# Attention layer: VectorE's checks reordered around the degrees, with four adj buffers; rank-decay layer: counts of two blocks made ahead of the layer norm

## The chip, the cores and the metric

The kernel runs on one core of a Trainium2 chip. The metric is the device time of one execution in microseconds (us), shown as the median of three runs. A separate, profiled execution gives the trace from which all durations below are read.

## The reference

Four graph layers run in a row over 3327 nodes with 64 features and one adjacency matrix `adj` of zeros and ones. Each layer takes `h = relu(layernorm(x))` and adds its result to `x`.

```python
# layers 0 and 3: hyperbolic attention
adj_att = sigmoid(left[:, None] + right[None, :] + b) * adj
support = einsum('ij,ijd->id', adj_att, logmap(x[:, None], x[None, :]))
x = x + proj(expmap(x, support))
# layer 1: rank decay. The last 100 neighbours of a row count, each further one half as much
rank = cumsum(adj != 0, axis=1); deg = rank[:, -1:]; k = minimum(deg, 100)
w = mask * where(rank - (deg - k) > 0, 0.5 ** (k - pos), 0)
x = x + w @ (h @ weight) + bias
# layer 2: signed attention between two GRU cells, without the diagonal of adj
node_support = concat((A > 0) @ h, (A < 0) @ h)
x = x + d_edge * gru(node_support, h) + d_node * gru(gat(h, A, A), h)
```

For an adjacency of zeros and ones the attention of layer 2 becomes a sum over neighbours, scaled by a function of the node's degree. The kernel computes that short form, and checks beside it, on VectorE, that the matrix holds nothing but zeros and ones: it counts the zeros of each quarter block (`zeros`, line 1247) and adds the ones that it counts anyway. If the total is wrong, a general form of all layers runs afterwards. It doesn't run on this input.

## The kernel before

The 3327 nodes are padded to 26 blocks of 128. The matrix comes in transposed, as `adjT`. The program goes through the four layers one after the other. Layers 0 and 3 are `hyperbolic_series` (line 322), layer 1 is `plain_decay` (1273), layer 2 is `plain_gat` (1431).

**Order of the work.** Most of the work stands in blocks with an order written out by hand (`tc.manual_schedule(engines=...)`): inside such a block the named engines carry out their instructions in program order. Between blocks a planner decides; an instruction that nothing holds back may be put ahead of an earlier block's. One example matters: `table_of(f)` (line 117) loads a table of ScalarE functions by a tiny activation into the tile `spare`. The one on line 404, the first ScalarE instruction of layer 3's block, stands in ScalarE's queue amid layer 2, directly behind the `table_of` of line 1506. DMAs are issued by SyncE (SP) in its own queue; the load of a tile waits there until the buffer is free.

**Rank-decay layer.** The matrix is read in 52 steps `(c, b)`, a half of the columns each and 26 blocks of rows from the last to the first. A step reads one tile of 128x1664 floats (832 KB, `load`, seven buffers). VectorE turns it into an fp8 mask (`make_mask`, line 1326) and counts its zeros (1329, by line 1248), except for the thirteen steps listed in `LATE` (line 1240), whose zeros are counted in the next layer. The masks stay on chip for layers 2 and 3. For each of the two halves `o` of a step, TensorE adds to the running counts (`counts(k, o, after)`, line 1333), ScalarE makes the weights `2^-count` (`weights`, 1339), and TensorE completes the count (`counts(k, o, rest)`). `sums` (1350) multiplies the weights with `h`. The order is: masks of steps 0 and 1; the layer norm (`norm_relu`, 123: VectorE with two Squares on ScalarE, line 135, and `split2`, line 181); then the loop over steps (1386). `late` splits the other half of `h`. GpSimd adds the bias (1415) from step 3 on.

**Attention layer.** The thirteen tiles of `LATE` are read again into three `adj` buffers (1451 to 1455). After the layer norm, TensorE runs through the 26 blocks `b` from 25 to 0, 16 matmuls each (1518), into four banks `acc`. Between the blocks stand, by the table `todo`: `turn` (transposes of `h` and copies on ScalarE, 1476), `degrees(k)` for the four parts k (two matmuls that sum the diagonal, and a VectorE subtraction from `deg`, 1495), and `inverse` (1497): VectorE clamps `deg`, ScalarE takes Relu, Ln and Exp of it, and two VectorE instructions (1507, 1508) make the attention's factor in `deg`. Behind each even block VectorE gets one check, a zero count of one `LATE` tile. Then the GRUs run in eight units `u` (two cells by four column parts): `take(k)` (two copies on ScalarE, 1538, and a multiplication on VectorE, 1539), `take2` (1544), `products` (TensorE, 1553 and 1558), `sigmoids` (ScalarE, 1565), `before_tanh` (VectorE, 1571 and 1572), `tanh` (1575) and `state` (VectorE, 1582 to 1586).

**End of layers 0 and 3** (line 689 on): some fifty VectorE instructions on 128x26 tiles. In layer 3 `th` holds a tanh, a table of Sqrt is loaded behind it by an activation that reads `th` (740), and line 742 multiplies `th` in place.

Of the kernel before, what the change touches and what calls it, by code (L numbers as in the profile page):

```python
# [9 lines left out]
F32 = mybir.dt.float32  # L10
BF = mybir.dt.bfloat16
# [8 lines left out]
P = 128  # L20
T = 26
# [25 lines left out]
def tile_gnn4(ctx: ExitStack, tc: tile.TileContext, x, adjT, att0, b0, w1, bias1, w_gat, a_gat,  # L47
# [274 lines left out]
    def hyperbolic_series(r, params, ok, masks=None, done=None):  # L322
# [18 lines left out]
        with ExitStack() as st:  # L341
# [347 lines left out]
            with tc.tile_pool(name="hse", bufs=1) as tp:  # L689
# [28 lines left out]
                if r is None:  # L718


                    f = MIN_NORM
                    by, g = new("by"), new("g")
                    V.tensor_scalar(by, v2, -f * f, 1.0, op0=OP.mult, op1=OP.add)
                    V.tensor_scalar(g, by, MIN_NORM, None, op0=OP.max)
                    V.reciprocal(g, g)
                    V.tensor_mul(t, root, g)
                    A.activation(th, t, AF.Tanh)
                    V.tensor_mul(th, th, rr)
                    V.tensor_mul(y2, th, th)
                    stt(vh, vh, 2.0 * f, th, op0=OP.mult, op1=OP.mult)  # L730
                    V.tensor_mul(y2, y2, x2)
                    stt(d, v2, f * f, y2, op0=OP.mult, op1=OP.mult)
                else:

                    V.tensor_scalar(t, v2, 1e-8, None, op0=OP.max)
                    ti = inverse_root(tp, t, "ti")
                    V.tensor_mul(t, t, ti)
                    V.tensor_scalar(t, t, um, None, op0=OP.max)
                    A.activation(th, t, AF.Tanh)
                    table_of(AF.Sqrt, th[:, :1])  # L740
                    V.reciprocal(ti, t)
                    V.tensor_mul(th, th, ti)
                    V.tensor_mul(y2, th, th)
                    stt(vh, vh, 2.0, th, op0=OP.mult, op1=OP.mult)
                    V.tensor_mul(y2, y2, v2)
                    V.tensor_mul(d, y2, x2)
# [526 lines left out]
    def plain_decay(masks, zo, deg, wt, bias, gru, ball_of_r):  # L1273
# [11 lines left out]
        with ExitStack() as st:  # L1285
# [24 lines left out]
            with tc.tile_pool(name="pdacc", bufs=1, space=PSUM) as pa, tc.manual_schedule(  # L1310
# [11 lines left out]
                def make_mask(k):  # L1322
                    c, b = steps[k]
                    adj = adjs.pop(k)
                    mask = masks[b // 2].rearrange("p q (o s i) -> p q o s i", o=2, s=2)[:, b % 2, :, c, :]
                    V.tensor_scalar(mask, adj, 1.0, None, op0=OP.is_equal, saturate=False)  # L1326
                    if k not in LATE:
                        same = wk.tile([P, 2, CW], BF, name="same", bufs=1)
                        zeros(same, adj, zo[:, k:k + 1])
# [33 lines left out]
                        A.activation(outP[:, c * CW + h * BK:c * CW + (h + 1) * BK], acc[h], AF.Copy, scale=1.0 / SH)  # L1363


                K_ = len(steps)
                make_mask(0)
                make_mask(1)
                H = pers.tile([P, T, D], F32, name="H")

                def late():
# [9 lines left out]

                with tc.tile_pool(name="pdp", bufs=1) as tp:
                    norm_relu(tp, H, order=(1, 0), then=after_norm)
                for o in range(2):
                    cnt[o] = pa.tile([P, 2, 512], F32, name=f"cnt{o}")
                for k in range(K_ + 2):
                    c, b = steps[min(max(k, 0), K_ - 1)]
                    if 0 <= k < K_:
                        counts(k, 0, after)
                        weights(k, 0)  # L1390
                    if 0 <= k - 1 < K_:
                        counts(k - 1, 1, rest)
                        if steps[k - 1][1] == 0:
                            degrees(steps[k - 1][0], 1)
                    if 0 <= k < K_:
                        counts(k, 1, after)
                        weights(k, 1)
                    if 0 <= k - 1 < K_:
                        sums(k - 1)
                        if steps[k - 1][1] == 0:  # L1400
                            out_of(steps[k - 1][0])
                    if 0 <= k < K_:
                        counts(k, 0, rest)
                        if b == 0:
                            degrees(c, 0)
                    if k + 2 < K_:
                        make_mask(k + 2)
                        if k + AHEAD < K_:
                            load(k + AHEAD)
                    if k == 1:  # L1410
                        late()
                    if 3 <= k < 3 + T // 2:

                        ts = slice(2 * (k - 3), 2 * (k - 2))
                        G.tensor_tensor(X[:, ts, :], X[:, ts, :], bias[:, None, :].to_broadcast([P, 2, D]), op=OP.add)
                    if k == 3:
                        for _, bt, brz in gru:
                            G.tensor_tensor(brz, bt[:, :3], bt[:, 3:], op=OP.add)
                        ball_of_r()
                    if k in (T + 3, T + 6):  # L1420
                        t0 = k - T - 3
                        pt = pa.tile([P, 3, 2, D], F32, name=f"acc{t0 // 3}", bufs=2)
                        from_pairs(None, outP, add, wt, range(t0, t0 + 3), pt)
                    if k - 2 >= T:
                        b = steps[k - 2][1]
                        drop_diagonal(masks[b // 2][:, b % 2, :], b, 0, NP)
# [4 lines left out]
    def plain_gat(masks, zo, deg, first, wg, gru):  # L1431
# [8 lines left out]
        with ExitStack() as st:  # L1440
# [7 lines left out]
            wgT = pers.tile([D, D], F32, name="wgT")  # L1448
            hundred = pers.tile([P, 1], F32, name="hundred")
            V.memset(hundred, -100.0)  # L1450
            wk = st.enter_context(tc.tile_pool(name="pgl", bufs=3))
            late = []
            for k in LATE:
                late.append(wk.tile([P, 2, CW], F32, name="adj"))
                nc.sync.dma_start(late[-1], quarters(k))
            with tc.tile_pool(name="pgp", bufs=1) as tp, tc.tile_pool(name="pgacc", bufs=1, space=PSUM) as pa, \
                    tc.manual_schedule(engines={mybir.EngineType.Activation, mybir.EngineType.DVE,
                                                mybir.EngineType.PE}):
                def bank(k):
                    return pa.tile([P, 512], F32, name=f"bank{k}")  # L1460

                hn = tp.tile([P, T, D], F32, name="hn")
                norm_relu(tp, hn, H.rearrange("p k o d -> p o k d"), order=(1, 0),
                          then=lambda o: split2(*[p[:, :, o, :] for p in parts], H[:, :, o, :]))
# [20 lines left out]
                        for o in range(2):  # L1485
                            A.activation(xh[g][o][D:, cs], pt[o * D:(o + 1) * D, :n * P], AF.Copy)

                def degrees(k):

                    cs = slice(k * BK, (k + 1) * BK)  # L1490
                    dg = bank(6 + k % 2)[:, :BK]
                    for o in range(2):
                        PE.matmul(dg[o * D:(o + 1) * D, :], ones_bf[:, :D],
                                  diag[:, o * HP + k * BK:o * HP + (k + 1) * BK], start=True, stop=True)
                    V.tensor_sub(deg[:, cs], deg[:, cs], dg)

                def inverse():

                    few = hn.rearrange("p t d -> p (t d)")
                    r0 = tp.tile([P, T, D], F32, name="ln_sq").rearrange("p t d -> p (t d)")  # L1500
                    V.tensor_scalar(zo[:, 2 * T:], zo[:, 2 * T:], first, None, op0=OP.mult)
                    V.tensor_scalar(deg, deg, 1.0, None, op0=OP.max)
                    A.activation(few, deg, AF.Relu, bias=hundred, accum_out=ok[:, 3:])
                    A.activation(r0, deg, AF.Ln)
                    A.activation(r0, r0, AF.Exp, scale=-1.0)
                    table_of(AF.Sigmoid, r0[:, :1])
                    V.scalar_tensor_tensor(deg, deg, -1.0, r0, op0=OP.mult, op1=OP.mult)
                    V.scalar_tensor_tensor(deg, deg, 2.0, r0, op0=OP.add, op1=OP.mult)

                todo = {T - 4: lambda: turn(0), T - 6: lambda: degrees(0), T - 8: lambda: turn(4),  # L1510
                        T - 9: lambda: degrees(1), T - 11: lambda: turn(8), T - 12: lambda: degrees(2),
                        T - 14: lambda: turn(12), T - 15: lambda: degrees(3), T - 17: inverse}
                for b in range(T - 1, -1, -1):
                    mask = masks[b // 2][:, b % 2, :]
                    for i, w in enumerate([p[:, b % C2, b // C2, :] for p in parts]):
                        for k in range(C):
                            for o in range(2):
                                PE.matmul(acc[k][o * D:(o + 1) * D, :], w,  # L1518
                                          mask[:, o * HP + k * BK:o * HP + (k + 1) * BK],
                                          start=b == T - 1 and i == 0, stop=b == 0 and i == 1)  # L1520
                    if b in todo:
                        todo[b]()
                    if b % 2 == 0:
                        same = wk.tile([P, 2, CW], BF, name="same", bufs=1)
                        k = LATE[(T - 1 - b) // 2]
                        zeros(same, late.pop(0), zo[:, k:k + 1])

# [171 lines left out]
```

## Time and profile before

| | |
|---|---|
| median of three runs | 819.15 us (817.87 to 821.02) |
| profiled execution | 818.34 us, its span 816.6 us |
| VectorE (DVE) busy | 709.1 us, 87% of the span |
| TensorE (PE) / ScalarE (ACT) / GpSimd (POOL) busy | 659.8 / 576.2 / 416.1 us |
| layer 0, rank-decay layer | to 283.8 us; 283.9 to 428 us |
| attention layer, layer 3 | 428 to 531 us; 531 to the end |

Times in the trace are counted from the start of the span. A line of the timeline gives start, duration, engine, source line, operation, tiles, count, and in brackets the idle time of the engine before it with what ended it. In the lists of waits the columns are: who waited, on whose instruction, total us, times, longest. "issue" is time in which an engine waited for nothing that the profile shows.

### The profile page before, as it was taken

The page shows a single profiled execution, that of the slowest core. Times are in us where ns is not written, and L with a number is a line of the kernel's source. Part 1 is how long each engine was busy: PE and PEld are TensorE (multiplying, and loading weights), DVE is VectorE, ACT ScalarE, POOL GpSimd, SP SyncE. Part 2 cuts the span into 40 slices and gives each one's busy share as a digit, 9 for nine tenths or more (in the row PEclk, how much of TensorE's full clock was granted, in tenths as well). Part 3 has the DMA queues.
Part 4 walks back from the last instruction along what each step waited for, and adds up shares of the span by engine and source line. Part 5 has one row for each costly group of instructions (what it writes and reads, how often), then busy time and mean ns, then how long its engine had stood idle before and what let it go on. Part 6 is the DMA issues. An engine that isn't in the chain of part 4 may idle for free. (4 is left out here: it accounts for less than half of the span.)

```text
span 816.6 us, 11802 instructions
## 1 busy us (share of the span) xinstructions
PE 659.8 (81%) x4215; PEld 252.1 (31%) x4215; DVE 709.1 (87%) x985; ACT 576.2 (71%) x729; POOL 416.1 (51%) x296
## 2 busy tenths in 40 slices
PE   0799999999999049989993995427999999999960
PEld 0522233333332024435441651214222333333320
DVE  6789999989998899998967567996899999999976
ACT  2678888878886367777782575255888888888862
POOL 2299988989987050003120000004687777787730
PEclk9989999999999569999996997757999999999995
DMA  3567676776664739998913541001001001000001
GB/s 75 164 203 219 205 212 184 205 213 196 196 189 120 292 131 327 372 379 298 367 36 132 187 151 50 1 4 45 1 1 34 1 1 36 1 1 2 1 2 46
DMA packets 57621, 107.84 MB, mean 132 GB/s; under 512 B 8752, under 2 KB 33488, under 8 KB 57552
## 3 DMA queue, kind: packets, MB, share of 16 engines
q1 hardware_dynamic: 53200, 106.97, 40.5%
q10 hardware_dynamic: 4352, 0.02, 0.3%
q8 instruction: 35, 0.57, 0.3%
q14 instruction: 34, 0.28, 0.1%
HBM read 103.72 MB, written 0.88 MB: 128 GB/s over the span
## 5 line engine op out<-in xcount | busy, mean ns | idle before, releaser
L595 ACT ACTIVATE y<-slot,shift_c 128x768 f32<-128x768 f32 (+1 forms) x208 | 197.4, 949 | 68.4 <-ACT sig L575 48.6
L601 DVE TENSOR_TENSOR sig<-slot,sig 128x768 f32<-128x768 f32 (+1 forms) x208 | 213.2, 1025 | 23.3 <-POOL sig L577 2.1
L600 DVE SCALAR_TENSOR_TENSOR slot<-y,slot 128x768 f32<-128x768 f32 (+1 forms) x208 | 212.1, 1020 | 9.1 <-ACT y L595 9.0
L577 POOL TENSOR_TENSOR sig<-adj,sig 128x768 f32<-128x768 f32 (+1 forms) x104 | 201.9, 1962 | 28.1 <-ACT sig L575 26.0
L575 ACT ACTIVATE sig<-leftB,right 128x768 f32<-128x768 f32 (+1 forms) x208 | 204.1, 981 | 3.5 <-DVE bh L544 3.5
L577 POOL TENSOR_TENSOR sig<-mask,sig 128x768 f32<-128x768 fp8e4 (+1 forms) x104 | 174.6, 1680 | 61.6 <-ACT sig L575 57.6
L610 PE MATMUL slot<-sig,Xr 128*64 128x384 f32 (+1 forms) x832 | 188.3, 541 | 16.8 <-DVE sig L601 16.8
L588 PE MATMUL slot<-XC,XT 128*128 128x384 f16 (+1 forms) x416 | 142.9, 344 | 5.2 <-DVE sig L601 3.5
L589 PE MATMUL slot<-XF,XE 73*128 73x384 f16 (+1 forms) x416 | 142.0, 341 | 0.0
L1339 ACT ACTIVATE w<-cnt,ebias 128x832 bf16<-128x832 f32 x104 | 93.7, 950 | 30.7 <-PE cnt L1333 30.7
L1248 DVE TENSOR_SCALAR_CACHE_REDUCE same<-adj 128x1664 bf16<-128x1664 f32 x52 | 97.5, 1876 | 3.6 <-DMA adj<-in 3.4
L618 PE MATMUL slot<-sig,X 128*32 128x384 f32 (+1 forms) x832 | 96.0, 533 | 0.0
L610 PEld LDWEIGHTS slot<-sig,Xr 128*64 128x64 f32 x832 | 43.1, 135 | 122.5 <-DVE sig L601 83.4
L1333 PE MATMUL cnt<-mask,after 128*128 128x416 fp8e4 x208 | 54.8, 347 | 22.7 <-DVE mask L1326 19.8
L588 PEld LDWEIGHTS <-XT 128*128 128x128 f16 x416 | 40.8, 98 | 96.1 <-issue 70.7
L191 POOL TENSOR_TENSOR mask<-mask,offdiag 128x128 fp8e4<-128x128 fp8e4 x26 | 15.0, 594 | 97.9 <-PE cnt L1333 97.9
L1333 PE MATMUL cnt<-mask,rest 128*128 128x416 fp8e4 x208 | 54.7, 345 | 10.2 <-ACT w L1339 10.2
L400 POOL MEMSET X<- 128x832 f32 x2 | 1.6, 794 | 115.0 <-PE pt L1234 115.0
L1326 DVE TENSOR_SCALAR mask<-adj 128x1664 fp8e4<-128x1664 f32 x52 | 52.9, 1035 | 0.0
L589 PEld LDWEIGHTS <-XE 73*128 73x128 f16 x416 | 40.9, 98 | 33.6 <-issue 9.9
L1350 PE MATMUL acc<-w,h 128*64 128x416 bf16 x416 | 46.6, 345 | 0.0
L1518 PE MATMUL bank<-mask,h 128*64 128x416 fp8e4 x416 | 39.7, 348 | 0.0
(299 smaller groups left out, 521.8 us busy)
## 6 DMA issues: line engine op xcount, KB each, us to landing
adj<-in SPq DMA_DIRECT2D x65, 832.0 KB, 6.6
adj<-in SPq DMA_DIRECT2D x78, 384.0 KB, 3.9
adj<-in SPq DMA_DIRECT2D x27, 512.0 KB, 4.4
leftB<-left SPq DMA_DIRECT2D x6, 384.0 KB, 3.5
XC<-XT SPq DMA_DIRECT2D x12, 96.0 KB, 4.3
X<-in SPq DMA_DIRECT2D x2, 416.0 KB
out<-X SPq DMA_DIRECT2D x2, 416.0 KB, 2.4
XF<-XT SPq DMA_DIRECT2D x6, 96.0 KB, 2.6
```

The source lines that it names most:

```text
L575: A.activation(sig, leftB[c], AF.Sigmoid, bias=right[:, b:b + 1])
L577: G.tensor_tensor(sig, adj, sig, op=OP.mult)
L588: PE.matmul(L[:, o, :c[1] * P], XT[:, rows], XC[c][:, o, :], start=True, stop=False)
L589: PE.matmul(L[:, o, :c[1] * P], XE[:KE, rows], XF[c][:, o, :], start=False, stop=True)
L595: A.activation(ys[k], Ls[k][:, :, :c[1] * P], AF.Square, scale=-0.5 / SX ** 2, bias=shift_c)
L600: V.scalar_tensor_tensor(L, y, G3, L, op0=OP.add, op1=OP.mult)
L601: V.tensor_mul(sig, L, sig)
L610: PE.matmul(acc[c][o * D:(o + 1) * D, 0, :n], Xr[:, b, :], sigs[k][:, o, :], start=b == 0, stop=b == T - 1)
L618: PE.matmul(acc[c][q:q + 32, 1, :n], X0[:, b - 1 + i, :], w[:, o, :], start=b == 1, stop=b == T - 1, tile_position=(0, q))
L1248: V.tensor_scalar(same, adj, 0.0, 0.0, op0=OP.is_equal, op1=OP.add, accum_out=count)
L1333: PE.matmul(cnt[o][:, h, :BK], w, cols(k, o, h), start=w is after and steps[k][1] == T - 1, stop=True, skip_group_check=True)
L1339: A.activation(ws[k][:, o, :, :], cnt[o][:, :, :BK], AF.Exp, scale=-LN2, bias=ebias)
```

## The change

In the rank-decay layer the counts and weights of steps 0 and 1 are issued ahead of the layer norm. `counts_before(k)` holds the part of a step that both places share. The table of Exp is loaded ahead of it and that of Sqrt behind it; `after_norm` still loads Exp again. Behind the norm come `sums(0)`, the masks 2 and 3 and loads 7 and 8, and then the loop from step 2.

In the attention layer there are four `adj` buffers instead of three. The checks move: four behind block 24, then the degrees of parts 0 and 1 together behind block 20, three checks behind block 19, the degrees of parts 2 and 3 behind block 16, `inverse` behind block 15 (it was 9) with four checks between its clamp and line 1507, and the last two behind line 1508. `turn(8)` and `turn(12)` go to blocks 14 and 11. The layer norm's pool is closed before the GRUs' pool is opened.

In layer 3's end, the multiplication behind the tanh writes a tile of its own.

```diff
                     A.activation(th, t, AF.Tanh)
                     table_of(AF.Sqrt, th[:, :1])
                     V.reciprocal(ti, t)
-                    V.tensor_mul(th, th, ti)
+                    ta, th = th, new("th_t")
+                    V.tensor_mul(th, ta, ti)
...
-                make_mask(0)
-                make_mask(1)
+                for o in range(2):
+                    cnt[o] = pa.tile([P, 2, 512], F32, name=f"cnt{o}")
+                table_of(AF.Exp)
+
+                def counts_before(k):
+                    counts(k, 0, after)
+                    weights(k, 0)
+                    if k:
+                        counts(k - 1, 1, rest)
+                        if steps[k - 1][1] == 0:
+                            degrees(steps[k - 1][0], 1)
+                    counts(k, 1, after)
+                    weights(k, 1)
+
+                for k in range(2):
+                    make_mask(k)
+                    counts_before(k)
+                    counts(k, 0, rest)
+                table_of(AF.Sqrt)
...
                     norm_relu(tp, H, order=(1, 0), then=after_norm)
-                for k in range(K_ + 2):
...
+                sums(0)
+                for k in range(2):
+                    make_mask(k + 2)
+                    load(k + AHEAD)
+                for k in range(2, K_ + 2):
+                    c, b = steps[min(k, K_ - 1)]
+                    if k < K_:
+                        counts_before(k)
+                    elif k == K_:
                         counts(k - 1, 1, rest)
+                        degrees(steps[k - 1][0], 1)
...
-                    if k == 1:
+                    if k == 2:
                         late()
...
-            wk = st.enter_context(tc.tile_pool(name="pgl", bufs=3))
+            wk = st.enter_context(tc.tile_pool(name="pgl", bufs=4))
...
+                before = st.enter_context(ExitStack())
+                tp = before.enter_context(tc.tile_pool(name="pgn", bufs=1))
...
-                def degrees(k):
-
-                    cs = slice(k * BK, (k + 1) * BK)
+                def diagonal(k):
+
                     dg = bank(6 + k % 2)[:, :BK]
                     for o in range(2):
                         PE.matmul(dg[o * D:(o + 1) * D, :], ones_bf[:, :D],
                                   diag[:, o * HP + k * BK:o * HP + (k + 1) * BK], start=True, stop=True)
-                    V.tensor_sub(deg[:, cs], deg[:, cs], dg)
+                    return dg
+
+                def check(n=1):
+                    for _ in range(n):
+                        same = wk.tile([P, 2, CW], BF, name="same", bufs=1)
+                        k = LATE[len(LATE) - len(late)]
+                        zeros(same, late.pop(0), zo[:, k:k + 1])
+
+                def degrees(*ks):
+                    for k in ks:
+                        cs = slice(k * BK, (k + 1) * BK)
+                        V.tensor_sub(deg[:, cs], deg[:, cs], diagonal(k))
...
                     table_of(AF.Sigmoid, r0[:, :1])
+                    check(4)
                     V.scalar_tensor_tensor(deg, deg, -1.0, r0, op0=OP.mult, op1=OP.mult)
                     V.scalar_tensor_tensor(deg, deg, 2.0, r0, op0=OP.add, op1=OP.mult)
-
-                todo = {T - 4: lambda: turn(0), T - 6: lambda: degrees(0), T - 8: lambda: turn(4),
-                        T - 9: lambda: degrees(1), T - 11: lambda: turn(8), T - 12: lambda: degrees(2),
-                        T - 14: lambda: turn(12), T - 15: lambda: degrees(3), T - 17: inverse}
+                    check(len(late))
+
+
+                todo = {T - 2: lambda: check(4), T - 4: lambda: turn(0), T - 6: lambda: degrees(0, 1),
+                        T - 7: lambda: check(3), T - 8: lambda: turn(4), T - 10: lambda: degrees(2, 3),
+                        T - 11: inverse, T - 12: lambda: turn(8), T - 15: lambda: turn(12)}
...
-                    if b % 2 == 0:
-                        same = wk.tile([P, 2, CW], BF, name="same", bufs=1)
-                        k = LATE[(T - 1 - b) // 2]
-                        zeros(same, late.pop(0), zo[:, k:k + 1])
-
+
+                before.close()
+                tp = st.enter_context(tc.tile_pool(name="pgp", bufs=1))
```

More of the change, by code (lines that the diff above doesn't have):

```diff
@@ L1383, in plain_decay @@
                     norm_relu(tp, H, order=(1, 0), then=after_norm)
-                for o in range(2):
-                    cnt[o] = pa.tile([P, 2, 512], F32, name=f"cnt{o}")
-                for k in range(K_ + 2):
[L1387 to L1391, printed above, removed]
-                        counts(k - 1, 1, rest)
[L1393 to L1397, printed above, removed]
+                sums(0)
[7 more added lines that the diff above has]
+                    elif k == K_:
+                        counts(k - 1, 1, rest)
+                        degrees(steps[k - 1][0], 1)
                     if 0 <= k - 1 < K_:
@@ L1401, in plain_decay @@
                             out_of(steps[k - 1][0])
-                    if 0 <= k < K_:
+                    if k < K_:
                         counts(k, 0, rest)
@@ L1455, in plain_gat @@
                 nc.sync.dma_start(late[-1], quarters(k))
-            with tc.tile_pool(name="pgp", bufs=1) as tp, tc.tile_pool(name="pgacc", bufs=1, space=PSUM) as pa, \
+            with tc.tile_pool(name="pgacc", bufs=1, space=PSUM) as pa, \
                     tc.manual_schedule(engines={mybir.EngineType.Activation, mybir.EngineType.DVE,
```

## The prediction

> **What bounds the kernel now.** I read the page's chain first: VectorE carries 31% of the span, most of it in the main loops of layers 0 and 3, which the change leaves alone. So I went to the three places of the edits. The waits between 425 and 500 us (who, on whom: total, times, longest) show the attention layer:
>
> ```profile
> DVE deg L1495 <- PE bank L1493: 11.2, 4, 7.2
> PE bank L1553 <- DVE deg L1539: 10.0, 1, 10.0
> DVE deg L1507 <- ACT ln_sq L1505: 7.7, 1, 7.7
> ACT xh L1544 <- DVE deg L1539: 6.9, 1, 6.9
> DVE same L1248 <- DMA adj<-in: 3.4, 2, 2.3
> ```
>
> VectorE first waits 18.9 us for others (11.2 for degrees, 7.7 for the inverse), and later ScalarE and TensorE wait for it. The chain that ended last says what it does then (start, us, what):
>
> ```profile
> 484.53 1.90 DVE same L1248 x2
> 486.49 1.77 issue
> 488.37 7.13 DMA adj<-in
> 495.61 1.89 DVE same L1248 x2
> 498.16 3.04 PE bank L1553 x8
> ```
>
> TensorE's accumulation is over at 485.07. Line 1539 could then run, but five checks stand ahead of it and the last tile arrives at 495.6; it starts at 497.43. In the decay layer the timeline shows
>
> ```profile
> 283.85 1.96 DVE L1326 TENSOR_SCALAR mask<-adj 128x1664 fp8e4<-128x1664 f32 x2
> 288.97 1.83 ACT L135 ACTIVATE ln_sq<-H 128x832 f32<-128x832 f32 x2 [9.13 <-DVE H L134]
> 295.80 1.78 ACT L1339 ACTIVATE w<-cnt,ebias 128x832 bf16<-128x832 f32 x2
> 313.11 1.95 DVE L1326 TENSOR_SCALAR mask<-adj 128x1664 fp8e4<-128x1664 f32 x2
> 314.18 0.51 PE L1333 MATMUL cnt<-mask,after 128*128 128x416 fp8e4 x2 [0.24 <-DVE mask L1326]
> 317.13 1.80 ACT L1339 ACTIVATE w<-cnt,ebias 128x832 bf16<-128x832 f32 x2 [0.54 <-PE cnt L1333]
> ```
>
> VectorE has no idle time from the norm's end (298.1) to step 7's mask (313.1), and TensorE waits for its masks in steps 4 to 7. From step 7 on ScalarE and TensorE alternate at 2.336 us a step (317.13, 319.46, 321.80), while VectorE needs 9.16 us for four (322.27 to 331.43). In layer 3's end:
>
> ```profile
> 796.97 1.28 ACT L119 ACT_TABLE_LOAD   x1
> 798.27 0.20 ACT L119 ACTIVATE spare<-th 128x1 f32<-128x1 f32 x1
> 798.50 0.19 DVE L742 TENSOR_TENSOR th<-th,ti 128x26 f32<-128x26 f32 x1 [1.46 <-ACT spare L119]
> 801.93 0.23 ACT L109 ACTIVATE ns<-n 128x26 f32<-128x26 f32 x1 [3.46 <-DVE n L776]
> ```
>
> **What the Trainium skill says.** Perfetto Trace Analysis, Sequencer Loop: an instruction waits for its semaphores after it was pushed into its engine's queue. The trace agrees: line 1495's first instance held VectorE for 7.22 us though tiles to check had landed. ScalarE: Activation LUTs, What ACT_TABLE_LOAD costs: 1283 ns for the load, and 1380 ns of draining. The trace has 1.283 us, but no draining: line 1504's load starts at 474.98 and its activation at 476.27. TensorE: Matmul & The Clock Gate, What's actually happening: an idle TensorE falls to half its clock after about 3.4 us. The count matmuls are 0.345 us apart at 285 us, after 18.9 us of idling, and 0.175 us later.
>
> **Part 1, decay layer: a loss of 3.1 us.** The masks of steps 0 and 1 stay where they are. The first count starts at 285.08, as now; a cold pair and its hand-over take 0.93 us (297.44 to the weights at 298.37). The four weights would run from 286.0. Now they take from 295.80 to 300.71, 4.91 us with the counts between them, also cold; so they end at 290.9. ScalarE then loads Sqrt (1.28) and passes its activation (0.11): the Squares start at 292.3 instead of 288.97, 3.35 us late. VectorE has nothing else in its queue; sums, scaling, both halves of the norm and mask 2 shift by it. GpSimd's bias additions end at 301.3 and no longer overlap mask 2, which took 1.27 us beside them and takes 1.02 alone: -0.25. Sum +3.1.
>
> What is late next: the masks 2 to 7, so step 7's weights, now bound by mask 7, start at 317.9 instead of 314.79. The lead of two steps that TensorE and ScalarE gain ends in waits for masks. `late` behind mask 4 instead of mask 3 is still ahead of mask 7. Behind step 7 the ScalarE/TensorE cycle repeats unchanged, so nothing comes back. Loads 7 and 8 still need only masks 0 and 1; later ones shift with VectorE, as their use does. Bounds: four weights of 0.95 us less 0.05 overlap from 286.0, without waits, end at 289.6, so at least +1.8; if the load of Exp before the first weights is not covered, +4.4. Its cover is ScalarE's idle time from 279.84 to 286. If the planner puts this table load earlier, into layer 0's preparation, as it does with line 404's, a Sigmoid load follows; ScalarE idles there 3.60 and 2.12 us, and 1.73 before the first sigmoid. I take 0; without cover 1.5 each.
>
> **Part 2, attention layer: a gain of 8.4 us.** I count on today's clock, without the shift of part 1. A check is 1.92 us with its read of the sum (443.62 to 445.54). The four tiles load ahead, as three do now (issued from 425.4, moved by 434). Four checks: 443.6 to 451.3. TensorE reaches block 20's end at 454.3; with two degree parts the subtractions end at 455.8. Three checks to 461.6. Four more blocks (1.41 us each) and a turn: degrees 2 and 3 at 461.6 to 462.7, clamp to 463.8. ScalarE then takes what it takes now from 473.19 to 480.76, 7.6 us: to 471.4. VectorE does four checks meanwhile, to 471.5: they cover that wait. Lines 1507 and 1508 (3.8) to 475.3, two checks to 479.1. VectorE is free 6 us before TensorE's end at 485.07, which doesn't move: the same matmuls in the same number of pauses.
>
> Tiles: a load lands 4.9 to 6.5 us after its issue, and SP needs 0.54 for one. Tile 8 (counted from 0) is issued after check 4 at 457.7 and needed at 465.6; the others have as much time or more. So 7.0 of 7.9 us, no stall; one of up to 6 us would be covered.
>
> Then line 1539 runs by 487. Behind it waits ScalarE's `take2` (6.95 us now, to begin at 491.1 after its own copies), then two sigmoids with 0.70 and 0.77 us for products that were late for the same reason: 8.4 us. From there ScalarE has no gaps to lose. `turn(8)` and `turn(12)`, behind `inverse` in ScalarE's queue, are copied by 479. Closing the norm's pool makes the first gate wait for line 1508, done at 475. Bounds: 6.95 if the sigmoids keep their waits; 9.9 if everything follows `products` of unit 2, which TensorE can start at 492.1 instead of 502.03.
>
> **Part 3, layer 3's end: a gain of 1.4 us.** Line 742 no longer waits for the table's activation to have read `th`; it starts when line 741 ends, 797.07 instead of 798.50. The next Sqrt would come at 800.5; its table is there at 798.3. The chain of small VectorE instructions has no other wait, so all of it counts. Between 1.2 and 1.46.
>
> Sum: 3.1 - 8.4 - 1.4 = -6.7 us. The profiled execution has 818.34 us (span 816.6), which becomes 811.6; the median of the runs lies 0.8 above it: 819.15 - 6.7 = 812.4.
>
> **Rivals.**
> A second good case: part 1 costs nothing, as the Squares get in earlier or VectorE catches up later. For it: TensorE and ScalarE do lead. Against it: steps 4 to 7 wait for masks, and VectorE's margin behind is 9.34 - 9.16 = 0.18 us in four steps. It gives 819.15 - 9.8 = 809.3.
>
> Table loads come back: the planner puts layer 3's Sqrt load (now at 482.30, before the gates, forcing a Sigmoid load at 486.73) between the gates, or Exp onto layer 0's path. Two to three loads of 1.28 on ScalarE's path, or stalls of the checks that eat as much: +4, 816.4. For it: ScalarE's queue isn't in program order today. Against it: ScalarE is idle where that load becomes possible.
>
> Slower: checks starve. With checks ahead of degrees and `inverse`, a late tile now holds the degrees' chain too. For it: 3.4 us of waits for tiles today, just where two loads follow each other closely. The margin is 0.9 us a tile, and then the 6 us. From 17 us of stall (6 covered, 11 to eat the gain and the bound below), the kernel is slower than 823.3: nine reloads each near 2 us later than the slowest now. Against it: four buffers rather than three, and loads spread over 25 us. It gives 824.
>
> **Numbers.** Half a per cent, 4.1 us, is about what a measurement of this kernel can tell from no change: faster means under 815.05. My forecast has 0.62, the good rival 0.13, the tables 0.18, starving 0.07. Of the forecast's spread (1.5 us by the bounds) hardly any passes 815, so faster 0.75, same 0.18, slower 0.07. The range leaves out starving and the far ends of the others: 808.5 to 817.5.
>
> **What would show it.** Squares near 292.3, mask 7 near 316.2, and the decay layer's last weights 3 us later; otherwise part 1 fails. In the attention layer no check between TensorE's last L1518 and L1539, no `take2` wait of 7 us; tile waits there would mean starving. L742 without its 1.46 us wait. A changed layer 0 or 3 main loop would make me wrong by a cause that I have not priced.

## The result and the profile after

The kernel after takes 813.78 us (median of ten runs, 812.64 to 816.02), the kernel before, timed beside it, 819.53 (817.03 to 821.44): a ratio of 0.9936, 95% interval 0.9921 to 0.9952, or 5.2 us less (3.9 to 6.5). The ratio is that of the means; the medians differ by 5.75 us. Below, a difference of timed runs is such a ratio times some 819.5 us, with the kernel before timed anew beside each group of runs. The forecast was 6.7 less and 812.4 us. The span of the profiled execution fell from 816.6 to 810.9 us.

The lines behind line 1326 have moved: 1326 is now 1327 (mask), 1333 is 1334 (counts), 1339 is 1340 (weights), 1350 is 1351 (sums), 1248 is 1249 (check), 1495 is 1523 (degrees), 1518 is 1549 (the attention's matmuls), 1538 and 1539 are 1567 and 1568, 1544 is 1573, 1553 is 1582, 1565 is 1594, 742 is 743.

I divided both traces at the same instructions and compared the pieces. A piece runs from one mark to the next (the start of the instruction, where no end is named).

| from – to | before, us | after, us | difference |
|---|---|---|---|
| start – mask of step 0 (layer 0) | 283.85 | 284.98 | +1.13 |
| – mask of step 7 (counts ahead of the norm) | 29.26 | 32.28 | +3.02 |
| – last weights of the decay layer | 109.03 | 110.39 | +1.36 |
| – first attention matmul, line 1518 or 1549 | 21.49 | 21.49 | 0.00 |
| – first instruction of layer 3, line 413 | 87.50 | 78.09 | -9.41 |
| – last instruction of line 653, behind layer 3's main loop | 261.56 | 261.35 | -0.21 |
| – end of the last addition to X (line 742's wait lies here) | 18.11 | 16.74 | -1.37 |
| – end of the span | 5.8 | 5.6 | -0.2 |
| span | 816.6 | 810.9 | -5.7 |

**Attention layer.** The list of waits of the kernel after between 428 and 500 us (who, on whom: total, times, longest):

```profile
DVE deg L1568 <- ACT xh L1567: 10.4, 4, 6.7
...
ACT xh L1567 <- PE bank L1549: 5.9, 1, 5.9
...
DVE deg L1523 <- PE bank L1510: 3.0, 1, 3.0
PEld bank L1587 <- DVE deg L1568: 2.8, 1, 2.8
...
PE bank L1587 <- DVE deg L1568: 2.1, 1, 2.1
```

VectorE's 11.2 us for degrees are 3.0, and TensorE's 10.0 are 2.1 (2.8 for its weight loads, PEld). VectorE's 7.7 for the inverse and its 3.4 for tiles are gone, and so are ScalarE's 6.9 in `take2`. Of VectorE's new 10.4, the longest, 6.7, is the wait for the end of the accumulation, on the other side of the checks; the other three are for ScalarE's copies. The timeline of VectorE around that end:

```profile
480.11 1.88 DVE L1249 TENSOR_SCALAR_CACHE_REDUCE same<-adj 128x1664 bf16<-128x1664 f32 x1
...
482.03 1.89 DVE L1249 TENSOR_SCALAR_CACHE_REDUCE same<-adj 128x1664 bf16<-128x1664 f32 x1
...
490.85 0.59 DVE L1568 SCALAR_TENSOR_TENSOR deg<-bank,deg 128x416 f32<-128x416 f32 x1 [6.68 <-ACT xh L1567]
491.92 0.59 DVE L1568 SCALAR_TENSOR_TENSOR deg<-bank,deg 128x416 f32<-128x416 f32 x1 [0.48 <-ACT xh L1567]
495.26 0.59 DVE L1568 SCALAR_TENSOR_TENSOR deg<-bank,deg 128x416 f32<-128x416 f32 x1 [2.75 <-ACT xh L1567]
496.32 0.59 DVE L1568 SCALAR_TENSOR_TENSOR deg<-bank,deg 128x416 f32<-128x416 f32 x1 [0.47 <-ACT xh L1567]
```

That of ScalarE, with the copies that VectorE waits for and the first `take2`:

```profile
489.76 2.13 ACT L1567 ACTIVATE xh<-bank 64x416 f32<-64x416 f32 x4 [5.94 <-PE bank L1549]
...
496.19 1.10 ACT L1573 ACTIVATE xh<-deg 64x416 f32<-64x416 f32 x2
```

The last check ends at 483.9, 6.3 us ahead of TensorE's end (490.24). In the chain that ended last the checks and the tile's landing, which held 484.5 to 497.4 before, have made room for TensorE and ScalarE (start, us, what):

```profile
474.65 15.09 PE bank L1549 x170
489.76 0.52 ACT xh L1567
...
495.77 0.52 ACT xh L1567
496.32 0.59 DVE deg L1568
```

**Decay layer.** VectorE's timeline, with the lines that answer to those of before:

```profile
284.98 1.96 DVE L1327 TENSOR_SCALAR mask<-adj 128x1664 fp8e4<-128x1664 f32 x2
...
294.35 1.95 DVE L137 TENSOR_REDUCE ln_v<-ln_sq 128x13 f32<-128x832 f32 x2 [3.35 <-ACT ln_sq L135]
...
317.26 1.96 DVE L1327 TENSOR_SCALAR mask<-adj 128x1664 fp8e4<-128x1664 f32 x2
```

And ScalarE's:

```profile
281.00 1.28 ACT L1340 ACT_TABLE_LOAD   x1
287.10 1.80 ACT L1340 ACTIVATE w<-cnt,ebias 128x832 bf16<-128x832 f32 x2 [4.82 <-PE cnt L1334]
...
292.04 1.28 ACT L119 ACT_TABLE_LOAD   x1
293.33 0.20 ACT L119 ACTIVATE spare<-one_c 128x1 f32<-128x1 f32 x1
293.44 1.67 ACT L135 ACTIVATE ln_sq<-H 128x832 f32<-128x832 f32 x2
```

The weights of two steps and a table load now stand ahead of the Squares, and VectorE has 3.35 us of idle time in front of line 137, where it had none. Mask 7 is 3.02 us later than before.

**Layer 0.** The timeline of ScalarE in its preparation:

```profile
21.14 1.28 ACT L119 ACT_TABLE_LOAD   x1
...
22.66 1.28 ACT L119 ACT_TABLE_LOAD   x1
...
35.73 1.28 ACT L575 ACT_TABLE_LOAD   x1 [1.71 <-DVE bh L544]
37.03 1.15 ACT L575 ACTIVATE sig<-leftB,right 128x1024 f32<-128x1024 f32 x1
```

The first load is Sigmoid's, as before. The second is the new Exp, which the planner has moved 260 us ahead of its place; it evicts Sigmoid, so a third load stands ahead of the first sigmoid (37.03; before 35.15). And it was of no use: the weights at 287.10 need Exp loaded once more, at 281.00.

**Layer 3's end.** Line 743 starts 0.10 us behind the end of line 741 (792.93), without a wait:

```profile
793.03 0.19 DVE L743 TENSOR_TENSOR th_t<-th,ti 128x26 f32<-128x26 f32 x1
```

### The profile page after: what moved, and what is told of

Read it like the earlier page. It is cut to its first block, busy times and chain, and to the rows that moved or that the text cites. A ratio compares the mean times of both kernels' runs of the same rounds, so it can differ in the third digit from the quotient of the medians.

```text
span 810.9 us, 11800 instructions
## 1 busy us (share of the span) xinstructions
PE 662.9 (82%) x4215; PEld 253.6 (31%) x4215; DVE 708.7 (87%) x985; ACT 581.7 (72%) x735; POOL 413.9 (51%) x296
## 5 line engine op out<-in xcount | busy, mean ns | idle before, releaser
L1351 PE MATMUL acc<-w,h 128*64 128x416 bf16 x416 | 48.8, 357 | 9.8 <-ACT h L183 9.3
```

## The experiments

I tested three claims: that the three parts add up and have the sizes given (against: one of them is free, or they collide); that the decay part's loss is the late Squares and the Exp load; that the attention part lives on the order of its checks and not on its fourth buffer. Marks of all runs, in us of one profiled execution each ("late weights" is the piece from mask 7 to the last weights):

| kernel | ratio to before [95%] | first sigmoid | mask 0 | mask 0 to mask 7 | late weights | first attention matmul to layer 3 |
|---|---|---|---|---|---|---|
| before | 1 | 35.15 | 283.85 | 29.26 | 109.03 | 87.50 |
| after | 0.9936 [0.9921, 0.9952] | 37.03 | 284.98 | 32.28 | 110.39 | 78.09 |
| attention part alone | 0.9879 [0.9859, 0.9899] | 35.26 | 284.24 | 29.27 | 109.03 | 78.30 |
| decay part alone | 1.0063 [1.0049, 1.0077] | 36.66 | 284.42 | 32.27 | 111.82 | 88.01 |
| own tile alone | 0.9987 [0.9976, 0.9999] | 35.82 | 284.36 | 29.27 | 110.49 | 86.77 |
| after, no Exp load ahead | 0.9904 [0.9887, 0.9921] | 35.23 | 283.46 | 32.27 | 110.54 | 78.15 |
| attention and tile | 0.9872 [0.9853, 0.9891] | 35.29 | 283.52 | 29.26 | 111.95 | 78.26 |
| after, three buffers | 0.9930 [0.9913, 0.9948] | 37.68 | 286.11 | 32.27 | 110.67 | 78.24 |
| after, one step ahead | 0.9896 [0.9870, 0.9922] | 37.60 | 286.03 | 29.54 | 111.90 | 78.21 |
| attention, tile, two more late checks | 0.9859 [0.9841, 0.9876] | 36.39 | 284.12 | – | – | 78.26 |

**The attention part alone.** The kernel before with the edits in `plain_gat` only.

```diff
-            wk = st.enter_context(tc.tile_pool(name="pgl", bufs=3))
+            wk = st.enter_context(tc.tile_pool(name="pgl", bufs=4))
...
-                todo = {T - 4: lambda: turn(0), T - 6: lambda: degrees(0), T - 8: lambda: turn(4),
+                todo = {T - 2: lambda: check(4), T - 4: lambda: turn(0), T - 6: lambda: degrees(0, 1),
...
```

> The kernel before with the attention layer's part alone. If the parts add up: the stretch from the first L1518 of the attention layer to layer 3's first reduction shrinks by 9.4 us, as between the two kernels, and nothing else moves: 9.4 us below before. Rival, that part of the 9.4 is a gain from the decay layer's shift (another clock or other DMA phase): 7 to 8.4 us, the figure of the prediction or less.

Measured: 809.47 us, 9.9 less than before (8.3 to 11.6). The stretch is 78.30 us, as in the kernel after. So the part's gain is real by itself, and the decay part in front of it doesn't change it: the interval of the times touches the rival's 7 to 8.4 us, but the stretch is 9.2 us shorter.

**The decay part alone.** The kernel before with the edits in `plain_decay` only (counts of steps 0 and 1, the two table loads, the loop from step 2).

```diff
+                table_of(AF.Exp)
...
+                for k in range(2):
+                    make_mask(k)
+                    counts_before(k)
+                    counts(k, 0, rest)
+                table_of(AF.Sqrt)
```

> The kernel before with the decay layer's part alone. Theory: slower by 1.1 us at the end of layer 0 (Exp's table load ahead of the main loop), by 3.0 at the mask of step 7, and by 0 to 1.4 at the change of columns, if TensorE's clock falls there as in the changed kernel's profile: 4.1 to 5.5 us above before. Rival, that the lead of two steps pays and something else in the whole change costs: 0 to 1 us, or below before.

Measured: 825.07 us, 5.2 more than before (4.0 to 6.3). Mask 7 is 3.0 us later, as in the kernel after. The rival in which this part is free has fallen.

**The tile alone.**

```diff
-                    V.tensor_mul(th, th, ti)
+                    ta, th = th, new("th_t")
+                    V.tensor_mul(th, ta, ti)
```

> The kernel before with the tile of its own for the scaled tanh in layer 3's end alone: 1.4 us below before, by the 1.46 us wait at line 742 that goes. Rival, that the next Sqrt activation waits for the table in its place: 0.

Measured: 818.48 us, 1.1 less (0.1 to 2.0). The three parts alone give -9.9 + 5.2 - 1.1 = -5.8 us; together they give -5.2. They add up within the intervals.

**Without the Exp load ahead of the counts.** The kernel after without that one line.

```diff
-                table_of(AF.Exp)
```

> The changed kernel without its explicit load of Exp ahead of the counts (the weights then load it on demand, in ScalarE's idle time behind layer 0). Theory: layer 0 ends 1.1 us earlier, as before the change, and the weights start no later: 1.1 us below the changed kernel, near 812.7. Rival, that the load on demand comes late and delays the first weights by 1.3: as the changed kernel or 0.2 above.

Measured: 811.47 us, a ratio of 0.9904 against 0.9936, 2.6 us less (give or take 1.9 by the two intervals; 1.1 was expected); the spans differ by 1.3. ScalarE's timeline of this kernel shows that the first sigmoid again needs no load of its own:

```profile
21.18 1.28 ACT L119 ACT_TABLE_LOAD   x1
...
35.23 1.15 ACT L575 ACTIVATE sig<-leftB,right 128x1024 f32<-128x1024 f32 x1 [1.73 <-DVE bh L544]
```

The price can be read a second way: mask 0 comes at 285.4 us on average in the four kernels with the load ahead (284.98, 284.42, 286.11, 286.03) and at 283.9 in the six without (283.85, 284.24, 284.36, 283.46, 283.52, 284.12). That is 1.5 us for a line that the kernel doesn't need.

**Attention and tile, without the decay part.** The kernel before with the diffs of the first and the third experiment.

> The kernel before with the attention layer's part and layer 3's tile, without the decay layer's part. Theory, the parts add up: -9.4 - 1.4 = 10.8 us below before, 808.6, and some 5 us below the changed kernel. Rival, that the decay layer's part is needed for the attention layer's gain (its shift of DMAs or clock): no better than the changed kernel, 813.8.

Measured: 809.47 us against 820.32 for the kernel before beside it, 0.9872, 10.5 less than before; against the kernel after (0.9936) the decay part costs 5.2 us here too.

**Three buffers.**

```diff
-            wk = st.enter_context(tc.tile_pool(name="pgl", bufs=4))
+            wk = st.enter_context(tc.tile_pool(name="pgl", bufs=3))
```

> The changed kernel with three adj buffers in the attention layer. Theory, the order of the checks makes the gain: each tile is then requested one check later; the fourth check waits about 2.6 us for its tile, which the wait for the degrees behind it takes up, and the last checks end 2 to 4 us later, inside the 6 us that VectorE is early: the same as the changed kernel within 0.5 us. Rival, the fourth buffer makes it: checks reach past the end of TensorE's sums, 3 us or more above the changed kernel.

Measured: 814.27 us, 0.9930, the same as the kernel after. VectorE's timeline in this kernel shows the waits for tiles, five of them with 4.4 us in all; these are the two longest, and the last check:

```profile
473.56 1.89 DVE L1249 TENSOR_SCALAR_CACHE_REDUCE same<-adj 128x1664 bf16<-128x1664 f32 x1 [1.38 <-DMA adj<-in]
...
478.96 1.89 DVE L1249 TENSOR_SCALAR_CACHE_REDUCE same<-adj 128x1664 bf16<-128x1664 f32 x1 [1.39 <-DMA adj<-in]
...
486.42 1.89 DVE L1249 TENSOR_SCALAR_CACHE_REDUCE same<-adj 128x1664 bf16<-128x1664 f32 x1
```

The last check ends at 488.3, TensorE at 491.79: the cover of 6.3 us has shrunk to 3.5 and is still enough. (The fourth check waited 1.23 us, not 2.6.) The fourth buffer buys margin and no time; the rest of the part makes the gain. What the rest consists of (the order of the checks, the paired degrees, the earlier `inverse`, the later `turn`s, the closing of the norm's pool) was not tried piece by piece; that the order of the checks carries most of it is read from the waits that went. The run also shows that stalls of VectorE of this size before TensorE's end are covered.

**One step ahead instead of two.** In the kernel after, only step 0 is counted ahead of the norm; the loop behind it starts a step earlier, so the order of masks and sums there changes too.

```diff
-                for k in range(2):
-                    make_mask(k)
-                    counts_before(k)
-                    counts(k, 0, rest)
+                make_mask(0)
+                counts_before(0)
+                counts(0, 0, rest)
+                make_mask(1)
...
-                sums(0)
-                for k in range(2):
-                    make_mask(k + 2)
-                    load(k + AHEAD)
-                for k in range(2, K_ + 2):
+                make_mask(2)
+                load(AHEAD)
+                for k in range(1, K_ + 2):
```

> The changed kernel with the counts and weights of step 0 alone ahead of the norm (step 1's mask stays there). Theory, the loss is the time that the weights hold up the norm's Squares: two weights end at 287.8 and Sqrt is loaded by 289.2, so the Squares are 0.25 us late instead of 3.35, from the first mask to step 7's 29.5 us instead of 32.3: 2.8 to 3.1 us below the changed kernel, near 811. Rival, that the loss comes from the order of masks and sums behind the norm or from a cold TensorE: 32.3 stays, and the time is the changed kernel's.

Measured: 812.64 us, 0.9896 against 0.9936, 3.3 us less than the kernel after (give or take 2.5), and mask 0 to mask 7 takes 29.54 us. The six runs lie far apart, from 808.59 to 814.50, and the profile is of one at 814.26, so the pieces of the trace say more here than the time. ScalarE's timeline:

```profile
288.15 1.80 ACT L1340 ACTIVATE w<-cnt,ebias 128x832 bf16<-128x832 f32 x2 [4.82 <-PE cnt L1334]
289.97 1.28 ACT L119 ACT_TABLE_LOAD   x1
...
291.37 1.67 ACT L135 ACTIVATE ln_sq<-H 128x832 f32<-128x832 f32 x2
```

The Squares start 5.34 us behind mask 0 (before 5.12, after 8.46), so one step's weights and the load fit into ScalarE's wait for the norm almost wholly, and the second step's don't. From the Squares to mask 7 it is 24.14 us before, 23.82 after and 24.20 here: the rival, a loss behind the norm, is not in the traces, though this run changed the order there as well. That places the 3 us of the decay part at the Squares.

**Two more checks moved out of the decay layer.** Attention and tile as above; steps 3 and 5 are added to the list, so the attention layer makes 15 checks.

```diff
-    LATE = 0, 1, *range(7, 2 * T - 4, 4)
+    LATE = 0, 1, 3, 5, *range(7, 2 * T - 4, 4)
```

> Attention layer's part and layer 3's tile without the decay layer's part, and the zero counts of steps 3 and 5 moved from the decay layer to the attention layer (15 checks there instead of 13). Theory: VectorE's masks bound steps 4 to 7 of the decay layer; without two checks of 1.88 us ScalarE and TensorE run at 2.336 us from step 2 on, step 7's weights start 1.6 us earlier, and the two checks fit into the 6 us that VectorE is early in the attention layer: 1.6 us below the run without this, near 807. Rival, VectorE has no such room in the attention layer, or the loads bound the decay layer: no gain or a loss of 2 us.

Measured: 808.30 us, 0.9859, the lowest of all, 11.6 us less than before; against attention and tile (0.9872) the intervals overlap, so the last 1.1 us aren't certain. The attention layer takes its 15 checks without loss (78.26 us in both). The trace says why the gain is less than 1.6. ScalarE's weights of steps 2 to 4 and 7:

```profile
303.06 1.80 ACT L1340 ACTIVATE w<-cnt,ebias 128x832 bf16<-128x832 f32 x2 [1.29 <-PE cnt L1334]
305.48 1.80 ACT L1340 ACTIVATE w<-cnt,ebias 128x832 bf16<-128x832 f32 x2 [0.63 <-PE cnt L1334]
307.82 1.80 ACT L1340 ACTIVATE w<-cnt,ebias 128x832 bf16<-128x832 f32 x2 [0.54 <-PE cnt L1334]
...
314.83 1.80 ACT L1340 ACTIVATE w<-cnt,ebias 128x832 bf16<-128x832 f32 x2 [0.54 <-PE cnt L1334]
```

From step 2 to step 7 they take 11.77 us, and TensorE no longer waits for a mask; in the attention part alone the same five steps take 13.39 (301.80 to 315.19). So the expected 1.6 us are there. But from the first weights to those of step 2 this execution took 6.99 us, the other 5.60: 1.39 more. The table of windows (length, busy time and count of TensorE, weight loads, VectorE, ScalarE, GpSimd, then TensorE's granted clock, DMA share, GB/s) has first this kernel,

```profile
297.00:303.00 6.00, 5.94 (x21) 2.26 (x21) 6.00 (x7) 3.55 (x5) 4.61 (x7) 0.50 0.05 7
```

and then the attention part alone:

```profile
297.00:303.00 6.00, 5.81 (x32) 2.44 (x31) 6.00 (x7) 4.78 (x7) 4.74 (x7) 0.75 0.03 3
```

TensorE came out of the norm's pause at half clock in both; here it stayed there for all 6 us, in the other for half of them (the clock came back at 302.95 and at 300.05 us).

## Why the prediction was right, and where it wasn't

**Part 1, the Squares: right.** The step said 3.35 us late, through the norm, less 0.25 for mask 2. Counted from mask 0, the Squares are at 8.46 instead of 5.12 us, +3.34, and mask 7 at 32.28 instead of 29.26, +3.02 (foretold +3.1). Mask 2 took 1.02 us, as foretold. Nothing came back in the steps behind.

**Part 1, the Exp load: wrong.** The step that failed is "I take 0; without cover 1.5 each". The page had shown ScalarE 1.73 us of idle time ahead of the first sigmoid, and I took that as cover for the Sigmoid load that an early Exp load would force. The planner did just what was named, but the new load of 1.28 us starts only when `bh` has landed, after 1.71 us of the idle time that should have hidden it. With 0.60 for `bh` itself, which came later by that, the first sigmoid is 1.88 late, and mask 0 then 1.13. Whether the 0.60 is the work of the Exp load is not shown: `bh` starts between 34.80 and 36.04 us in the six traces without it, and between 35.03 and 36.04 in the four with it. Over ten traces the mean at mask 0 is 1.5 us. The Trainium skill (ScalarE: Activation LUTs, What ACT_TABLE_LOAD costs) gives 1283 ns for a load, which both loads show. The trace before had no load behind a wait: the one at 271.51, for line 109, ran ahead of its activation's 2.14 us of waiting. This was half of the rival of the table loads.

**Part 1, the cycle behind step 7: wrong in one thing.** "Behind step 7 the ScalarE/TensorE cycle repeats unchanged" holds for the order, not for the pace. At the change from the first half of the columns to the second, TensorE waits twice for ScalarE's degrees, 1.04 and 1.85 us, before as after. After, its clock fell to half within the second pause, at 366.16 us:

```profile
363.98 0.51 PE L1334 MATMUL cnt<-mask,after 128*128 128x416 fp8e4 x2 [1.04 <-ACT deg L1356]
...
366.69 0.85 PE L1334 MATMUL cnt<-mask,after 128*128 128x416 fp8e4 x2 [1.85 <-ACT deg L1356]
367.47 1.60 PE L1351 MATMUL acc<-w,h 128*64 128x416 bf16 x8
```

In the kernel before the same sums took 0.89 us and this pair of counts 0.51. The loss is +1.36 us in the ledger. I don't put it down to the change: the profile of the kernel with the tile alone, which leaves this layer as it was, has it too (+1.46), and that of attention and tile has it twice over (+2.9); before, the attention part alone and the last experiment have none. All five profiles with some form of the decay part have it, two of five without. What decides in a single profile is worked out in the last section. Whether the part makes it more frequent stays open; ten profiles don't settle that. The timed difference that the decay part makes, 5.2 us twice, is 0.7 more than its 3.0 and 1.5, which is within the intervals and would also be the size of such a share.

**Part 2: right in its mechanism, 1 us too small.** Foretold -8.4 (6.95 to 9.9), measured -9.41; seven kernels with the part have 78.1 to 78.3 us, three without 86.8 to 88.0. The checks ended 6.3 us ahead of TensorE (foretold 6), without one wait for a tile, and `take2` began at 496.19, which is 491.0 when TensorE's later end (5.17 us) is taken off: foretold 491.1. Two details were off. "Line 1539 runs by 487" is so of its first instance only: each waits for ScalarE's two copies of the same bank, so the last starts at 496.32. It cost nothing, since ScalarE's own queue was the chain, but VectorE's freedom there was less than I wrote. And the gain splits in another way than I wrote. From the first attention matmul to the end of the last `state` instruction it is 7.90 us (83.27 to 75.37). Behind that, the update of X took 4.23 us before layer 3 could start (526.90 to 531.13) and takes 2.72 (524.51 to 527.23), since part of it now stands between the instructions of the last units. I had left the end of the stretch as it was; which piece of the part lets the update in between was not tried. One table load now counts that didn't before: layer 3's Sqrt load (482.33) still evicts Sigmoid ahead of the gates, and the load that brings it back, at 491.91, stands in the chain that ended last, where ScalarE has no idle time from 489.76 to `take2`. By its length I estimate that up to 1.3 us could be had with the Sqrt load behind the gates; no run tried it.

**Part 3: right.** The wait of 1.46 us is gone, and 1.37 of it is found in the ledger. By itself it measured 1.1 (0.1 to 2.0).

**The sum.** Of the forecast's -6.7: +1.13 for the Exp load and +1.36 for the clock were not in it, the attention's extra -1.0 neither, and the rest is 0.5 in small pieces. The range held because its terms erred in both directions; the sum's closeness, 1.4 us, owes something to that. The rival in which checks starve has fallen: even with three buffers the waits stayed under cover.

## What to carry to other kernels

Work put into an idle engine is free only while its end stays ahead of what stands behind it in the same queue: one step's weights and a table load fitted into ScalarE's wait, the second step's moved the layer norm by 3 us. When a block with an order of its own begins with an instruction that depends on nothing, look up where the planner puts it; here a "preload" ran 260 us early, evicted a table that was in use, and had to be loaded again anyway. Checks that nobody waits for belong where the engine would wait for others, and not ahead of an instruction that others wait for: the part built on that gave 9.4 us, and no buffer was needed for it.

## What the runs showed of the hardware

A table load isn't always hidden by the wait of the activation that needs it. The load at 35.73 us began when that activation's operand had come, after 1.71 us of idle time; the one at 281.00 ran while the same engine waited 4.82 us more for its counts. What makes the difference wasn't tried.

TensorE fell to half its clock at two pauses of 1.04 and 1.85 us with 0.86 us of matmuls between, in some profiles and not in others with the same pauses to a hundredth. The losses of the seven profiles come in two sizes, 1.4 to 1.6 us (four) and 2.8 to 2.9 (three). The granted clock, read in windows of 0.1 us, says why. In the kernel after it changes at 270.59, 291.07, 294.48, 308.14, 366.16 and 369.58 us. These distances are 6, 1, 4, 17 and 1 times 3.413 us. The other traces have the same interval, each with its own starting point; cut along it, none of the ten has an interval that holds both clocks. The half-clock spell at the change of columns is one interval (3.41 us) in the four profiles and two (6.83) in the three.

What counts is how the pauses fall on the intervals. In the kernel after, most of both lie in one, and the clock falls in the next (columns as in the table of windows above):

```profile
362.75:366.16 3.41, 1.05 (x6) 0.38 (x4) 3.41 (x5) 2.60 (x5) 0.00 (x0) 1.00 1.00 370
366.16:369.58 3.42, 2.89 (x12) 0.93 (x12) 3.42 (x6) 2.30 (x5) 0.00 (x0) 0.50 1.03 406
```

In the kernel before, they are divided between two, and it doesn't fall:

```profile
357.90:361.32 3.42, 1.70 (x12) 0.59 (x7) 3.42 (x5) 2.63 (x4) 0.00 (x0) 1.00 0.99 339
361.32:364.73 3.41, 2.25 (x16) 1.05 (x16) 3.41 (x4) 2.77 (x7) 0.00 (x0) 1.00 1.00 380
```

At this place, TensorE was busy for 0.86 to 1.48 us of the interval ahead of the fall in the seven profiles, and for at least 1.70 us of every interval in the three that didn't fall. The Trainium skill (TensorE: Matmul & The Clock Gate, What's actually happening) says that the clock is decided over windows of about 3.4 us that run freely; the traces agree, with 3.413 us. For a reader of profiles it means that a difference of 1.4 or 2.9 us between two single profiles with pauses of this size can be the clock alone.
